# Attention in a planned order, a rearranged last routing chain, and fifteen weight halves loaded ahead

## The chip, the cores and the metric

The kernel runs on one core of a Trainium2 chip. It is one launch that holds a whole two-layer network for a batch of 16 images. The metric is device time in microseconds; the number of a kernel is the median over its runs. A profile is taken of one execution, and its times are counted from the start of that execution's span.

## The reference, cut to what matters

The input `x` has 16 samples of 128 channels x 32 x 32 points, so N = 1024 points per sample. All data are 32-bit floats.

```
x = x + attention(_ln_c(x))              # layer 0: 4 heads, linear attention:
                                         #   group norm over the sample, q,k,v = w_qkv xn
                                         #   q = softmax over points, k = softmax over channels of a head
                                         #   context = k v^T, out = context^T q, y = w_out out + b_out
t = tokens(x)
t = t + stu(_ln_t(t))                    # spectral filters (FFT convolution with K filters) + 3 taps,
                                         #   four lengths mixed by a softmax / one-hot of 4 weights
x = from_tokens(t)
x = x + relu(bn(conv3x3(relu(bn(conv3x3(_ln_c(x)))))) + residual)     # layer 1
t = tokens(x)
t = t + experts(_ln_t(t))                # 64 experts, each picks its 8 best of the 1024 tokens,
                                         #   pools them, 128 -> 512 -> 128 with a gelu,
                                         #   and adds its result back to those tokens
```

## The kernel before

The program goes through four stages, one after the other on the same core.

Stage A is the attention of layer 0 with all that the spectral part needs of each sample. A sample goes through some sixty named operations: `tokens` (TensorE turns x to tokens, eight 128x128 transposes, L152), `moments` and `root` and `scales` (mean and deviation per token, on DVE L135, ACT L121 and DVE L127 to L129), `norm` (ACT, L144, eight pieces), `channels` (TensorE turns back, L172), `channels_copy` (ACT L424), `group` (the group norm's scale, L402), `q` (L433) and `k` (L451) with their softmaxes, `q_tokens`, `context` (L499), `fold` and `fold2`, `out` (L534), `out_add`, `input` (L157), the second norm, `even` and `odd` (L571: the spectrum by even and odd parts), butterflies on POOL (L287 to L309) and the store of the spectrum `vd` (L628); beside it `taps_in`, `taps` (L639, 24 matmuls) and `taps_add` (L646), whose result is stored to `xd` (L647). The ACT copies between a TensorE result in PSUM and the next step are `tokens_copy` and `input_copy` (L550). In PSUM there are three buffers "big" (128x1024) and two "s" (small).

The order of A's work is written out by hand: `period` is a list of names with an offset each, and a loop over p from -6 to 15 issues every name for sample p + offset. TensorE, DVE, ACT and POOL execute in this order (their queues are pinned); the order on SP, which issues most DMAs, is left to the framework. Two generators are advanced once per period: `filters()` (the filters' own spectrum, L652 and L657, and the loading and mixing of M_phi) and `prepare()` (conv weights, on POOL). Where TensorE would be idle, `keep()` puts warm-up matmuls that compute nothing (L165):

```
idle = {("tokens", 1): 5, ("filters", 0): 4, ("channels", 0): 1, ("k", 1): 2}
```

At the start, DVE also prepares the taps' weights `mu` (L337, L339), whose DMA goes through POOL's queue.

Stage B is the spectral multiplication: per chunk of frequencies the samples' spectrum `xc` is fetched from `vd` (L793), turned on POOL, and multiplied with generated filters `g` (generate L817, copies L828 on DVE and L830 on ACT, multiply L841).

Stage C is the two convolutions. Its order comes from `planned()`, a list scheduler in the program: a table gives each operation an engine, a cost, a due time, what it depends on and the buffers it takes and frees; the scheduler issues the operation that is due and can run. Some operations of the last samples are moved by hand after that (`move`). Each sample ends in the routing of the experts: norm (`scales2`, `norm20`, `norm21`), `channels`, `logits` (L1320), the choice of eight tokens (L1341, L1344, for the last sample L1473 to L1485), the turning of the gates (`turn`, L1413 for the last sample, and its copy `turn_copy`), `pool` (L1367) and `pooled` (L1380, L1384). The last sample has a class of its own, `Final`, which works in halves. Conv's last steps on DVE and POOL are `sums2`, `ends2` (POOL L1222), `mids2` (L1226), `rows2` (L1232) and `last` (L1422, L1426).

Stage D is the experts. Of the 32 weight halves (1 MB each, 16 groups of experts with two halves) 14 are loaded ahead into a ring of tags whose buffers have become free (`RING`, `load_half`); half 2g+14 is issued after `hidden(g)` (L1684; biases before it, L1675) and half 2g+13 after `output(g-1)` (L1709), and behind the weights the five pairs of x that were put away (`AWAY`, xb) are reloaded. At the end the experts' outputs are turned (L1746), added up per pair of samples (`ob`, L1751), spread over the tokens with the gates (L1769, into `pfy`), added to x (L1779) and stored to the output.

Of the kernel before, what the change touches and what calls it, by code (L numbers as in the profile page):

```python
# [69 lines left out]
def metaformer_kernel(ctx: ExitStack, tc: tile.TileContext, io: dict, out: bass.AP):  # L70
# [106 lines left out]
    with ExitStack() as l0:  # L177
# [43 lines left out]
        with ExitStack() as a0:  # L221
            aconst = a0.enter_context(tc.tile_pool(name="aconst", bufs=1))
            setup = a0.enter_context(tc.tile_pool(name="setup", bufs=2))
            work = a0.enter_context(tc.tile_pool(name="awork", bufs=2))


            spool = a0.enter_context(tc.tile_pool(name="spool", bufs=2))
            xpool = a0.enter_context(tc.tile_pool(name="xpool", bufs=8))
            ppool = a0.enter_context(tc.tile_pool(name="ppool", bufs=1))
            ps = a0.enter_context(tc.tile_pool(name="aps", bufs=2, space=PSUM))  # L230
# [120 lines left out]
            def small(shape, name):  # L351
                return work.tile(shape, F32, name=name, tag=name, bufs=5)

            idle = {("tokens", 1): 5, ("filters", 0): 4, ("channels", 0): 1, ("k", 1): 2}

            class Attention:
# [10 lines left out]
                def tokens(self):  # L367
                    if self.b + 2 < B:
                        load(self.b + 2)
                    self.x = xt[self.b]  # L370
                    self.pt = big().rearrange("p (j c) -> p j c", c=C)
                    transpose_in(self.pt, self.x)

                def tokens_copy(self):
                    self.tok = work.tile([P, NT, C], F32, name="tok", tag="tok", bufs=3)
                    nc.scalar.copy(self.tok, self.pt)
# [171 lines left out]
                def input_copy(self):  # L548
                    self.ub = work.tile([P, NT, C], F32, name="ub", tag="ub")
                    nc.scalar.copy(self.ub, self.pt)  # L550
# [74 lines left out]
                def odd_turns4(self):  # L625
                    butterflies(self.ao, self.xf, 1, self.sd)
                    for cs in (slice(0, 1), slice(1, NCH)) if self.b + 1 == B else (slice(NCH),):
                        nc.sync.dma_start(  # L628
                            vd[cs, :, self.b, :].rearrange("c p w -> p c w"),
                            self.xf[:, cs].rearrange("p c x r m j -> p c (x r m j)"),  # L630
                        )
# [13 lines left out]
                def taps_add(self):  # L645
                    nc.vector.tensor_tensor(self.x, self.pa, self.x, ALU.add)  # L646
                    nc.sync.dma_start(xd[self.b], self.x)  # L647

            def filters():

                wfm = setup.tile([P, NQ // 2, 2 * P], F32, name="wfm", tag="mi")
                nc.vector.tensor_scalar(wfm, wf[:, 1::2, :], -1.0, None, ALU.mult)  # L652

                def values(q, dst):
                    for sgn in range(2):
                        w = wfm[:, q // 2, :] if sgn and q % 2 else wf[:, q, :]
# [4 lines left out]
                yield  # L661
                xf = spectrum_tile()
                for parity in range(2):
                    pe = class_values(parity, values)
                    t = class_copy(pe, 1)
                    ts = class_copy(pe, ROT) if parity else t
                    ab = class_sums(parity, pe, t)
                    class_differences(parity, ab, pe, ts)
                    yield
                    for part in range(2):  # L670
                        butterflies(ab, xf, parity, part)
                    if parity:
                        butterflies(ab, xf, 1, butterflies(ab, xf, 1, 2))
                    yield
                half = CW // 2
                e, o = (xf[:, :, i].rearrange("p c r m j -> p c (r m j)") for i in range(2))
                nc.vector.tensor_tensor(ph[:, :, :half], e, o, ALU.add)
                nc.vector.tensor_tensor(ph[:, :, half:], e, o, ALU.subtract)
                for m in range(EPR // MB):
                    es = slice(m * MB, (m + 1) * MB)  # L680
                    for i in range(NF):
                        mi = setup.tile([P, MB, C], F32, name="mi", tag="mi")
                        nc.sync.dma_start(mi, io["M_phi"][i, :, es, :])
                        yield
                        if i == 0:
                            nc.vector.tensor_scalar(mst[:, es, :], mi, coef[:, 0:1], None, ALU.mult)
                        else:
                            nc.vector.scalar_tensor_tensor(
                                mst[:, es, :], mi, coef[:, i : i + 1], mst[:, es, :], ALU.mult, ALU.add
                            )  # L690

            def prepare():
# [4 lines left out]
                for n in range(2):  # L697
# [20 lines left out]
                    for k, r, f in ((0, 0, 24.0), (1, 2, 6.0), (2, 1, 12.0)):  # L718
                        eng.tensor_scalar(cw[:, :, k], raw[:, :, r], 1.0 / f, None, ALU.mult)
                    eng.tensor_tensor(cw[:, :, 0], cw[:, :, 0], cw[:, :, 1], ALU.add)  # L720
# [4 lines left out]
                for n in range(2):  # L725
# [4 lines left out]
                    for si, (lo, hi) in enumerate(SEGS[1:], 1):  # L730
                        ws = w[:, :, :, lo // NQ : hi // NQ]
                        eng.tensor_scalar(ws, ws, seg[:, NF - 1 - si : NF - si], None, ALU.mult)
                        if si > 1:
                            yield
                    nc.sync.dma_start(wid[:, qs], w)

            nc.sync.dma_start(wf, io["wf"])
            phi = spool.tile([P, NQ, 2, P], F32, name="phi", tag="xf")
            nc.sync.dma_start(phi, io["phi"])


            period = (
                ("q_max", 3), ("out_add", 1), ("tokens", 6), ("moments", 6), ("context", 2),
                ("channels", 4), ("input", 1), ("norm2", 0), ("context_mask", 2),
                ("group_root", 4), ("k_exp", 3), ("fold", 2), ("group_scale", 4), ("moments2", 1),
                ("q_exp", 3), ("even", 0), ("tokens_copy", 6), ("taps_in", 0), ("input_copy", 1),
                ("channels_copy", 4), ("filters", 0), ("fold_copy", 2), ("even_copy", 0),
                ("even_sums", 0), ("taps_copy", 0), ("odd", 0), ("even_turns", 0),
                ("variance2", 1), ("root2", 1), ("q_tokens", 3), ("scales", 5), ("fold2", 2),
                ("q_copy", 3), ("k_sum", 3), ("scales2", 1), ("root", 6), ("spread", 5),  # L750
                ("k_recip", 3), ("k", 4), ("even_turns2", 0), ("q_recip", 3), ("variance", 6),
                ("fold2_copy", 2), ("odd_copy", 0), ("taps", 0), ("odd_sums", 0), ("k_max", 4),
                ("odd_scaled", 0), ("k_scale", 3), ("norm", 5), ("group", 5), ("odd_sums2", 0),
                ("q", 4), ("odd_turns", 0), ("taps_add", 0), ("odd_turns2", 0), ("out", 2),
                ("group_var", 5), ("odd_turns3", 0), ("k_sub", 4), ("odd_turns4", 0),
            )
            reach = max(d for _, d in period)
            samples, setting, preparing = {}, filters(), prepare()
            with tc.manual_schedule(engines=PINNED):
                for p in range(-reach, B):  # L760
                    next(preparing, None)
                    for name, d in period:
                        b = p + d
                        if name == "filters":
                            next(setting, None)
                            keep(ps, "s", idle.pop((name, 0), 0) if p > -reach else 0)
                        elif 0 <= b < B:
                            if name == "tokens":
                                samples[b] = Attention(b)
                            getattr(samples[b], "q_" if name == "q" else name)()  # L770
                            keep(ps, "s", idle.get((name, b), 0))
                assert next(preparing, None) is None
                for _ in setting:
                    pass
# [160 lines left out]
    with ExitStack() as c1:  # L935
# [12 lines left out]
            "y", "wi", "z", "y", "cw0", "v", "cw1", "p1", "yo",  # L948
        )
        FIRST = ("wi", "v", "cw0", "cw1", "p1", "y")  # L950
        halves = {}

        def load_half(h):

            g, n = divmod(h, 2)
            es, tag = slice(g * EG, (g + 1) * EG), RING[h % len(RING)]
            if g >= E // EG:
                pr = AWAY[0] + h - 2 * (E // EG)
                if pr in AWAY:
                    tag = RING[(pr - AWAY[0] + 18) % len(RING)]  # L960
                    pool = first if tag in FIRST else xpool if tag[:2] == "xp" else work
                    x = pool.tile([P, 2, N], F32, name=f"xb{pr}", tag=tag, bufs=RING.count(tag))
                    for j in range(2):
                        xt[2 * pr + j] = x[:, j]
                        nc.sync.dma_start(x[:, j], xd[2 * pr + j])
                return
            pool = first if tag in FIRST else xpool if tag[:2] == "xp" else work
            w = pool.tile([P, EG * HID], F32, name=f"we{n}", tag=tag, bufs=RING.count(tag))
            if n == 0:
                nc.sync.dma_start(  # L970
                    w.rearrange("p (e h) -> p e h", e=EG), w1[es, 0:C, :].rearrange("e d h -> d e h")
                )
            else:
                nc.sync.dma_start(
# [961 lines left out]
```

## Time and profile before

| what | value |
|---|---|
| median of 3 runs | 1227.47 us (1225.88 to 1232.86) |
| profiled execution | 1229.05 us, span 1227.0 us |
| granted TensorE clock, mean | 0.988 |
| stage A: last taps matmuls / last butterfly on POOL end | 384.1 / 386.65 us |
| taps of three samples in a row begin at (L639) | 194.98, 216.30, 237.63 us |
| first k matmuls (L451) | 29.22 us |
| first hidden layer of the experts (L1684) | 1137.65 us |
| last expert output matmuls (L1709) | 1192.81 us |
| first output store issued / last stores issued | 1202.81 / 1218.65 us |

PE is TensorE's matmuls and PEld its weight loads, DVE is VectorE, ACT is ScalarE, POOL is GpSimd and SP is SyncE. A line of a timeline has start, duration (all in us), engine, line in the program, operation, output and inputs by the program's names, sizes and how many such instructions stand together; the bracket tells how long the engine stood idle before it and what ended that. A wait line tells which engine waited for which work: us in total, how often, and the longest.

### The profile page before, as it was taken

The page shows a single profiled execution, that of the slowest core. Times are in us where ns is not written, and L with a number is a line of the kernel's source. Part 1 is how long each engine was busy: PE and PEld are TensorE (multiplying, and loading weights), DVE is VectorE, ACT ScalarE, POOL GpSimd, SP SyncE. Part 2 cuts the span into 40 slices and gives each one's busy share as a digit, 9 for nine tenths or more (in the row PEclk, how much of TensorE's full clock was granted, in tenths as well). Part 3 has the DMA queues.
Part 4 walks back from the last instruction along what each step waited for, and adds up shares of the span by engine and source line. Part 5 has one row for each costly group of instructions (what it writes and reads, how often), then busy time and mean ns, then how long its engine had stood idle before and what let it go on. Part 6 is the DMA issues. An engine that isn't in the chain of part 4 may idle for free.

```text
span 1227.0 us, 34351 instructions
## 1 busy us (share of the span) xinstructions
PE 1155.2 (94%) x14364; PEld 946.8 (77%) x14364; DVE 932.7 (76%) x1956; ACT 721.2 (59%) x1414; POOL 602.2 (49%) x800
## 2 busy tenths in 40 slices
PE   6889999999999999999997999999999999998996
PEld 4677767777677899998996888888888888885453
DVE  5888888887767677777764689898888989877335
ACT  4777777776656777877760445555555555554211
POOL 2436454664568788888882433343333333230003
PEclk9999999999999999999998999999999999999998
DMA  7004435243446244344348511233233322416998
GB/s 283 24 31 158 133 99 173 87 160 124 132 142 182 81 141 139 137 139 140 125 147 282 134 52 52 87 103 120 80 121 112 103 86 70 155 35 237 357 404 341
DMA packets 91243, 175.14 MB, mean 143 GB/s; under 512 B 5968, under 2 KB 42064, under 8 KB 90448
## 3 DMA queue, kind: packets, MB, share of 16 engines
q1 hardware_dynamic: 90448, 170.46, 41.1%
q0 software_dynamic: 640, 2.49, 0.6%
q8 instruction: 113, 1.85, 0.6%
q14 instruction: 42, 0.34, 0.1%
HBM read 110.28 MB, written 62.65 MB: 141 GB/s over the span
## 4 chain that ended last, share of the span: by engine, by line
PE 52%; DVE 22%; issue 10%; ACT 5%; DMA 5%; POOL 5%; SPq 0%; POOLq 0%; DVEq 0%; ACTq 0%
PE pcv L1013 10%; PE py L841 8%; PE pg L817 8%; PE big L639 6%; DVE bst L135 4%; PE big L172 3%; PE big L152 3%; PE big L571 3%; PE big L451 2%; PE big L534 2%; PE big L433 2%; DVE abss L1256 1%; DVE xp L1278 1%; DVE xp L1140 1%; POOL v L808 1%
## 5 line engine op out<-in xcount | busy, mean ns | idle before, releaser
L1013 PE MATMUL pcv<-v,cw 128*128 128x256 f32 x1152 | 258.2, 380 | 1.6 <-POOL v L1203 1.6
L1013 PEld LDWEIGHTS pcv<-v,cw 128*128 128x128 f32 x1152 | 214.7, 190 | 34.7 <-issue 4.9
L828 DVE COPY g<-pg 128x512 f32<-128x512 f32 x196 | 127.6, 682 | 67.9 <-PE pg L817 67.9
L830 ACT COPY g<-pg 128x512 f32<-128x512 f32 x316 | 161.1, 606 | 28.7 <-PE pg L817 27.9
L817 PE MATMUL pg<-ph,mst 32*128 32x128 f32 x4096 | 138.9, 278 | 1.4 <-DVE x L646 0.9
L817 PEld LDWEIGHTS pg<-ph,mst 32*128 32x128 f32 x4096 | 125.9, 187 | 15.6 <-DVE g L828 8.3
L841 PE MATMUL py<-g,v 128*32 128x128 f32 x4096 | 126.0, 276 | 1.9 <-POOL v L809 1.6
L841 PEld LDWEIGHTS py<-g,v 128*32 128x32 f32 x4096 | 109.2, 110 | 9.7 <-POOL v L809 2.1
L144 ACT ACTIVATE tok<-tok,sts 128x128 f32<-128x128 f32 x256 | 101.9, 480 | 16.9 <-DVE sts L1090 13.6
L135 DVE BATCH_NORM_STATS2 bst<-big 128x6 f32<-128x256 f32 x252 | 89.6, 416 | 19.9 <-PE big L152 10.7
L808 POOL TENSOR_TENSOR v<-xc 128x256 f32<-128x256 f32 x128 | 98.0, 790 | 9.9 <-DMA xc<-vd 9.2
L639 PE MATMUL big<-u,mu 128*128 128x128 f32 (+4 forms) x384 | 86.0, 380 | 0.0
L1203 POOL TENSOR_TENSOR v<-abss 128x256 f32<-128x256 f32 x64 | 49.1, 787 | 68.2 <-DVE abss L1199 56.8
L287 POOL TENSOR_TENSOR xf<-ab 128x256 f32<-128x256 f32 x34 | 24.8, 728 | 112.6 <-DVE ab L254 112.5
L1222 POOL TENSOR_TENSOR yo<-abss 128x256 f32<-128x256 f32 x32 | 23.5, 734 | 107.5 <-DVE abss L1218 107.5
L639 PEld LDWEIGHTS big<-u,mu 128*128 128x128 f32 x384 | 56.7, 191 | 18.0 <-issue 15.4
L571 PE MATMUL big<-wf,ub 128*128 128x256 f32 x256 | 63.5, 392 | 0.2
L809 POOL TENSOR_SCALAR v<-v 128x256 f32<-128x256 f32 x64 | 55.0, 860 | 5.6
L476 POOL TENSOR_TENSOR ke<-ke,ks 128x1024 f32<-128x1024 f32 x16 | 30.6, 1913 | 54.9 <-DVE qs L484 43.2
L144 ACT ACTIVATE tt<-tt,sts 128x128 f32<-128x128 f32 x120 | 47.8, 481 | 13.9 <-DVE sts L1090 13.9
L571 PEld LDWEIGHTS big<-wf,ub 128*128 128x128 f32 x256 | 47.0, 193 | 9.1 <-ACT xn L424 3.0
L915 ACT COPY yt<-py 128x512 f32<-128x512 f32 x60 | 35.1, 585 | 31.2 <-ACT g L830 17.6
(277 smaller groups left out, 2479.8 us busy)
## 6 DMA issues: line engine op xcount, KB each, us to landing
we<-in_weight SPq DMA_DIRECT2D x32, 1024.0 KB, 9.1
xc<-vd SPq DMA_DIRECT2D x64, 256.0 KB, 3.0
yd<-ys SPq DMA_DIRECT2D x32, 512.0 KB, 3.6
vd<-xf SPq DMA_DIRECT2D x15, 1024.0 KB, 5.1
y<-yd SPq DMA_DIRECT2D x15, 896.0 KB, 6.1
x<-in_x SPq DMA_DIRECT2D x16, 512.0 KB, 5.5
mi<-in_M_phi SPq DMA_DIRECT2D x16, 512.0 KB, 4.7
xd<-x SPq DMA_DIRECT2D x16, 512.0 KB, 6.2
```

Source lines behind the costliest of these rows:

```text
L135: nc.vector.bn_stats(bst[:, j : j + 2, :].rearrange("p j s -> p (j s)"), src[:, j : j + 2, :].rearrange("p j c -> p c j"),)
L144: nc.scalar.activation(dst[:, j, :], src[:, j, :], AF.Identity, bias=nm[:, j : j + 1], scale=r[:, j : j + 1],)
L571: nc.tensor.matmul(dst, self.ub[:, q, :], wf[:, q, :], start=True, stop=True)
L639: nc.tensor.matmul(self.pa[:, a:hi], mu[:, NF - 1 - si, tap, :], self.u[:, a - tap : hi - tap], start=(tap == 0), stop=(tap == KU - 1),)
L808: nc.gpsimd.tensor_tensor(vv[:, x, 1:, bs], e, o, op)
L809: nc.gpsimd.tensor_scalar(v[:, :, 0, bs], v[:, :, 2, bs], -1.0, None, ALU.mult)
L817: nc.tensor.matmul(pg[r][:, i], mst[rs, 4 * q + i, :], ph[rs, c, :], start=True, stop=True,)
L828: nc.vector.tensor_copy(dst, src)
L830: nc.scalar.copy(dst, src)
L841: nc.tensor.matmul(py[rows, x, kl, :], v[:, (x * NM + m) * JL + jl, 1 - ri : 3 - ri, :] .rearrange("p k b -> p (k b)"), g[:, ((x * 2 + ri) ...
L1013: nc.tensor.matmul(pc[:, i], wt[:, dy, k, :], v[:, k, dy * WT : dy * WT + HT], start=(dy == 0), stop=(dy == 2),)
L1203: nc.gpsimd.tensor_tensor(v[:, k, WT : WT + HT], self.ab[:, 0], self.ab[:, 1], op)
```

## The change

Three stages are touched.

In stage A `period` and the two generators are replaced by the list scheduler of stage C, with a table of all operations of a sample, the filters' steps (`f_...`, now a class `Filters`) and the preparation's (`p_...`), and earliest times for the loads. All of A's warm-up matmuls go. The loads of x for samples 2 to 7 are issued at the start, interleaved with wf and phi: x0, x1, x2, x3, wf, x4, x5, phi, x6, x7. `tokens_copy` and `input_copy` are done in two halves. Small tiles have 7 buffers instead of 5. The last sample's spectrum store is one chunk on SP and 15 on ACT's queue, and its x is stored from ACT's queue too.

In stage C, `scales2` of sample 14 is done by POOL (six operations) instead of DVE (four) and is moved behind `ends2`; the copy of sample 13's turned gates is put ahead of sample 14's norm; the last sample's norm is four pieces on DVE and four on ACT instead of five and three. Of the seven warm-ups of two matmuls behind the last `logits` two are left, and the biases of the first two expert groups are put into PSUM there.

In stage D fifteen weight halves are loaded ahead. The added one lies in two quarters behind the halves in the tags "z" and "v". After that, whenever a half is used up, the next of a list is loaded: first all weights, then the five pairs of x. The four warm-ups of two matmuls behind the last transposes go. The first pair of samples is added and stored in halves of 512 points.

The diff, cut to its core:

```diff
-                    nc.scalar.copy(self.tok, self.pt)
+                    for h in range(2):
+                        js = slice(h * NT // 2, (h + 1) * NT // 2)
+                        nc.scalar.copy(self.tok[:, js], self.pt[:, js])
...
-            idle = {("tokens", 1): 5, ("filters", 0): 4, ("channels", 0): 1, ("k", 1): 2}
+            idle = {("begin", 0): 0}
...
-                    nc.sync.dma_start(xd[self.b], self.x)
+                    (nc.sync if self.b + 1 < B else nc.scalar).dma_start(xd[self.b], self.x)
...
+            for b in range(2, 4):
+                load(b)
             nc.sync.dma_start(wf, io["wf"])
+            for b in range(4, 6):
+                load(b)
             phi = spool.tile([P, NQ, 2, P], F32, name="phi", tag="xf")
             nc.sync.dma_start(phi, io["phi"])
+            for b in range(6, 8):
+                load(b)
...
-            period = (
-                ("q_max", 3), ("out_add", 1), ("tokens", 6), ("moments", 6), ("context", 2),
...
+            table = (
+                ("load", "SP", 1.28, 2153.3, "", "x", ""),
+                ("tokens", "PE", 0.88, 4110.1, "load", "big:t tok", ""),
+                ("moments", "DVE", 1.337, -1802.8, "tokens~.6", "", "big:t"),
+                ("tokens_copy", "ACT", 1.034, 110.7, "tokens moments~.7", "", "big:t"),
...
+                ("channels_copy", "ACT", 1.114, -1271, "channels group_scale", "xn", "big:c"),
+                ("q", "PE", 1.78, 1191.3, "channels_copy", "big:q", ""),
...
+                ("k", "PE", 1.8, -1013.3, "channels_copy", "big:k", ""),
...
+                ("taps", "PE", 5.22, 6831.9, "taps_copy", "big:ta", "u"),
...
+            order = planned(
+                table, buffers, B, 520.01, lambda b, name: b > 0 and name[:2] in ("f_", "p_"),
+                lambda b, name: START.get((b, name), START.get(name, 0.0)),
+            )
...
         RING = tuple(f"xp{pr}" for pr in AWAY) + (
-            "y", "wi", "z", "y", "cw0", "v", "cw1", "p1", "yo",
+            "y", "wi", "z", "y", "rest", "cw0", "v", "cw1", "p1", "yo",
         )
...
+        pending = [h for g in range(E // EG + 1) for h in (2 * g, 2 * g - 1)]
+        pending = [h for h in pending if len(RING) <= h < 2 * E // EG]
+        pending += [2 * E // EG + i for i in range(len(AWAY))]
...
-        idle = {(13, "turn"): 4, (13, "pooled"): 2, (15, "logits"): 7, (15, "turn"): 1}
+        idle = {(13, "turn"): 4, (13, "pooled"): 2, (15, "logits"): 2, (15, "turn"): 1}
...
+        class Other(Routed):
...
+            def scales2(self):
+                g = nc.gpsimd
+                r, a, t, nm = (self.sts[:, i, :] for i in range(4))
+                g.tensor_tensor(t, r, r, ALU.mult)
+                g.tensor_tensor(t, t, a, ALU.mult)
+                g.tensor_scalar(t, t, -0.5, 1.5, ALU.mult, ALU.add)
+                g.tensor_tensor(r, t, r, ALU.mult)
+                g.tensor_tensor(nm, self.m, r, ALU.mult)
+                g.tensor_scalar(nm, nm, -1.0, None, ALU.mult)
...
-        move((d, "scales2"), behind=(e, "mids2"))
+        move((d, "scales2"), behind=(e, "ends2"))
...
+        move((d - 1, "turn_copy"), ahead=(d, "norm20"))
...
+                if b == B - 1 and name == "logits":
+                    for g in range(2):
+                        phs[g] = ps.tile([P, HID], F32, name="ph", tag="cv", bufs=3)
+                    biases(0)
...
-                    load_half(2 * g + len(RING))
+                    freed(2 * g)
...
-            keep(ps, "cv", 4)
...
+                for hf in range(2 if pr == 0 else 0):
+                    cs = slice(hf * HALF, (hf + 1) * HALF)
+                    for b in range(2):
+                        nc.vector.tensor_tensor(xt[b][:, cs], py[b][:, cs], xt[b][:, cs], ALU.add)
+                        nc.sync.dma_start(outs[b][:, cs], xt[b][:, cs])
```

## Prediction

> **What bounds the kernel now.** I read the busy rows and the 40 slices first, then windows by stage, then the waits of one stretch and the timeline of single periods. The profiled execution took 1229.05 us, 1.6 above the median of the runs shown (1227.47); its span is 1227.0 and 2.05 us lie around it. Sums are made against 1229.05; 1.6 comes off at the end.
>
> ```profile
> PE 1155.2 (94%) x14364; PEld 946.8 (77%) x14364; DVE 932.7 (76%) x1956; ACT 721.2 (59%) x1414; POOL 602.2 (49%) x800
> PE   6889999999999999999997999999999999998996
> DMA  7004435243446244344348511233233322416998
> ```
>
> TensorE has work for 94% of the span; DMA fills its slices only at the very end. So there are two regimes: up to about 1140 us TensorE's order and its holes set the pace, after that the transfers do.
>
> Stage A (attention) ends with the last taps matmul at 384.1 and POOL's last butterfly at 386.65. By windows (columns: window, length, busy time and count of PE, weight loads, DVE, ACT, POOL, then clock, DMA share, GB/s):
>
> ```profile
> 0.00:80.00 80.00, 64.34 (x405) 46.62 (x406) 59.39 (x191) 52.75 (x110) 25.55 (x36) 0.98 0.34 123
> 120.00:248.00 128.00, 123.94 (x862) 94.84 (x858) 106.61 (x260) 95.50 (x200) 66.51 (x104) 1.00 0.40 127
> 335.00:385.00 50.00, 47.69 (x268) 36.00 (x266) 33.25 (x62) 24.92 (x50) 34.90 (x61) 1.00 0.47 149
> 195.00:216.30 21.30, 20.62 (x144) 15.77 (x143) 17.86 (x43) 15.89 (x34) 11.71 (x18) 1.00 0.43 133
> ```
>
> One period is 21.3 us with 20.62 of TensorE work: the steady state has no more than 0.7 us per sample to give. The poor part is the ramp: 15.7 us idle in the first 80 and the 64.3 busy contain 10.3 us of warm-up matmuls (24 at 0.43) that compute nothing. The steady hole is one wait:
>
> ```profile
> 210.48 1.09 PE L172 MATMUL big<-ident,ub 128*128 128x128 f32 x8 [0.67 <-ACT ub L550]
> PE big L172 <- ACT ub L550: 9.2, 11, 1.6
> ```
>
> At the end:
>
> ```profile
> 1128.24 3.29 PE L165 MATMUL wm<-ident 128*128 128x256 f32 x14
> 1131.89 1.05 PE L1675 MATMUL ph<-b,ident 32*32 32x512 f32 x4
> 1192.81 1.08 PE L1709 MATMUL peo<-we,ht 128*32 128x128 f32 x32 [1.63 <-DMA we<-in_weight]
> 1196.71 2.76 PE L165 MATMUL wm<-ident 128*128 128x256 f32 x8
> 1195.00:1200.00 5.00, 4.94 (x18) 3.94 (x20) 2.16 (x8) 0.00 (x0) 0.00 (x0) 0.66 1.03 420
> 1200.00:1205.00 5.00, 5.00 (x23) 2.09 (x20) 3.45 (x3) 1.01 (x1) 0.55 (x1) 1.00 0.53 217
> ```
>
> Warm-up matmuls stand in line with the last routing chain; the last weight half is waited for 1.63 us; the transfers run full until 1200 and then only half full for 5 us, since the first output is not yet added up. From 1205 on 8.4 MB of outputs at about 400 GB/s are the rest (21 us).
>
> **Part 1, stage A in a planned order: −17 us.**
> *Work that stays.* All matmuls of the samples remain: 16 x 20.65 (123.94 over 6 periods) = 330.5, and the filter values, two groups of 16 (3.69 us each) = 7.4; together 338.
> *Work that goes.* 24 warm-ups, 10.3 us. They fill idle time at the ramp, so the gain comes only where real work takes their place:
> *Ramp.* The first transposes run at 7.5 in both (x lands then). The four mu operations stay where they hold DVE until mu lands (before: L337 at 14.04, the last L339 ends at 17.0), then scales, norm on ACT (3.2), channels (1.7) and the group's scale; the first k, at 29.22 before, comes at about 26.5, because the filters' sums no longer lie in front of the first sample's scales (DVE L254, L267, 20.43 to 21.7). Of the 19 us up to there TensorE has about 8.5 of useful work (10.5 lost); 6 more are lost, I estimate, until enough samples are in flight: 16.5 (before: 15.7 and 10.3 of warm-ups in 0:80). So 7.5 + 16.5 + 338 = 362.
> *Small stalls.* Busy time in A (0 to 385) is 356.7 in all; less the 10.3 it is 346.4, 8 above 338, since lone matmuls show their latency. In a denser stream I keep some of it: +5. TensorE ends at 367 instead of 384.1, and POOL's last butterfly 2.5 behind as before. So −17. If the ramp loses nothing beyond the start, and no stall stays: −27. If it keeps before's 0.67 per sample and the ramp is no better than 20 lost: about −8.
> *Other queues.* SP now issues x2 and x3 ahead of wf, and x4, x5 ahead of phi; before the phi landed at 15.95 and its matmuls waited for it (0.80). Four loads of 0.5 MB at 400 GB/s put it 5 us later, at 21; the values (3.7) stand ahead of the first k in TensorE's queue and end at 24.7, before k's input: 0, and +2 in the range if phi is later. If mu (on POOL's queue, 9.6 us to land before) is slowed by this traffic, DVE's whole queue stands behind it, x0's scales and norm first: 0 to +3, in the range; I take 0, as x's loads ran beside it before too. The two ACT copies per sample are each split in halves: 32 more instructions (1024-wide 1.01, 512-wide 0.58: 0.3 per sample on an engine busy 15.9 of 21.3): nothing while TensorE leads, and the half that comes first lets its reader begin earlier. Seven small buffers for five only remove waits.
> *The seam.* For the last sample vd's other 15 chunks and x's store go onto ACT's queue: two issues of about 0.4 us ahead of g's copies, which wait for POOL's last butterfly in both programs; 0 to +1, taken as 0.5 and contained in the 5. xc's first three fetches now stand behind vd's first chunk on SP (before they were issued at 380.43, ahead of it), but the fourth (xc at 391.61, 5.45 to land) came last before as well: 0, with ±2 in the range.
>
> *A rule against it.* Granted clock with the warm-ups: 0.98 in 0:80; after the waits of 1190 to 1195, 0.66 in 1195:1200. The Trainium skill (TensorE: Matmul & The Clock Gate, Part 1: The HAM clock gate) says that TensorE is granted only half its clock until it has been busy for some 3.4 us. By the rule, dropping the warm-ups makes the first transposes, the 3.7 us of filter values and the first k groups slower, up to +4 us at the ramp, and A gives −13. The row's 0.98 says nothing for a program without them. I take +1, inside the 5, since the first work after the transposes waits for mu and phi anyway; +4 stays in the range.
>
> **Part 2, last routing chain: −2.75.** Of the warm-ups behind the last logits (14 matmuls, 3.29 us from 1128.24, 0.235 each) 4 remain (0.9), and the 16 bias matmuls of the first expert pair (4 x about 0.27 = 1.05) come here, where TensorE waits for the exp and the gates (DVE L1485 ends at 1131.2) anyway. In before the flips follow at 1131.37, and the bias group of 1.05 stands between the two flips, 12 more (1.07) behind the pooling. Gone from the path: 0.75 of warm-ups past the gates' end or its latency, 0.85 between the flips, 0.45 before ppt = 2.05.
> Scales2 of sample 14 leaves DVE: four operations, 1112.71 to 1113.45 = −0.74 on the engine that carries the chain (mids, rows, last, moments). It becomes six POOL operations, with no row but the kin L1294:
>
> ```profile
> L1294 POOL TENSOR_SCALAR sts<-bst x16: 196/250/1095, 726.4 to 1120.0; 128x8 f32<-128x8 f32 x16
> 1109.09 1.09 POOL L1294 TENSOR_SCALAR sts<-bst 128x8 f32<-128x8 f32 x1 [8.55 <-DVE bst L135]
> ```
>
> By the median 6 x 0.25 = 1.5, from ends2's end at 1111.81 to 1113.3: norm of sample 14 on ACT begins about where it did (1113.57). The long one of 1.09 lay beside a DVE operation with two inputs in SBUF (L1344, 1108.92 to 1110.13). The Trainium skill (GPSIMD Engine Reference, 8. Key points) has POOL share SBUF interfaces with VectorE and contend with such operations; mids, rows and last are of that kind. By the rule each of the six may be held: up to 6 x 1.09 = 6.5, end at 1118.3, norm (3.19) ends at 1121.5, channels (1118.94) would start 2.5 late and its copy would hold ACT before the final norm. I go by the median and keep +2.5. Gtt's copy ahead of norm20 stands in that order on ACT already (1111.38 and 1113.57): 0. Four and four instead of five and three in the final norm: ACT starts when DVE's last is written (1.80 <- L1444), 4 x 0.336 + 4 x 0.39 = 2.9 against 2.83: 0.
>
> **Part 3, experts and outputs: −4.95 more.** The DMA stream of weights and x reloads sets the end from 1145 on (400 to 420 GB/s, share 1.05). It starts 2.75 earlier, and 1 MB is loaded ahead of it: at (15, inverse), when the slices show DMA at 0.4, into tiles that are free; 1 MB at 405 GB/s = 2.6. And the 2.35 us hole (5 us at 0.53) closes: TensorE's 8 warm-ups (2.76, 1196.71 to 1199.47, beside which DVE's ob sums run until 1199.1) go, the first pair is added and stored in halves, so the first store is issued about 1195 (before's clock) instead of 1202.81. With part 2: 2.75 + 2.6 + 2.35 = 7.7. The expert chain of TensorE (hidden 0 at 1137.65 to outputs at 1193.9, less the 1.63 wait, moved by 2.75) ends at about 1189.5, the added part (ot, ob, first half pair) some 6 us later: 1195.5, just when the stream ends. All weights now go ahead of all x reloads, which are needed from the second pair on, 3 us later: near, but covered. By the clock rule above, the first pair without warm-ups takes double (8 matmuls 1.99 and 1.88): +1.9. Range of parts 2 and 3: −3.5 to −9.
>
> **Sum.** −17 − 7.7 = −24.7: 1229.05 − 24.7 = 1204.35, less 1.6 = **1203**.
>
> **Rivals.** A measurement of this kernel tells about 0.5% (6.1 us): faster is below 1221.3, slower above 1233.6.
> 1. *The plan keeps holes.* Stage C's order comes from the same planner, and in 720:1060 TensorE waits 11 us of 340 (6.6 of them `PE big L172 <- DVE xp L1140`), 3.2%, just what A's hand-written period has (0.67 of 21.3). Then A gains only its ramp: −9; with 7.7, 1212.4, so **1211**. Against: in the new order each steady operation's input stands well ahead of it.
> 2. *The tail gives half.* Cold clock at the first pair or POOL held: parts 2 and 3 give −3.5 to −4, all in all −20.7: **1207**.
> 3. *Slower.* TensorE's queue is in order, with three "big" PSUM buffers between it and the ACT and DVE copies. In the planned order k follows the channels' copy, and fold the mask, with a few tenths of us; if the real copies come later than planned, TensorE stalls in every sample. It decides from 24.7/16 = 1.54 us per sample, a period of 22.2 against 20.65; at 2.3 per sample (16 x 2.3 = 36.8) **1239.5**. For: seven of the waits behind C's 6.6 us are of this kind. Against: DVE (17.9) and ACT (15.9) have 3 to 5 us free in a period.
> 4. *No change*: the same at 1.2 to 1.9 per sample, 1227.
>
> **Chances.** Forecast 0.60, rival 1 0.17, rival 2 0.10 (all faster: 0.87), no change 0.05, slower 0.08. Range: down to 1191 (A −27, tail −9: 1193, less 1.6), up to 1216 (rival 1 with the late mu and a cold ramp); no change and slower are left out.
>
> **What would show it.** Right: taps every 20.7 to 20.9 us from the fifth sample on, POOL's last butterfly near 369, the last L1709 near 1172 without a wait for we, DMA share near 1 through the first stores. Wrong: waits of L451, L433 or L571 on ACT or DVE in each period (rival 1 or 3); L1294-like POOL operations of 1 us and a late norm of sample 14; pfy at 1.9 for eight with a DMA share of 0.5 ahead of the first store (rival 2).

## The result, and the profile after

The changed kernel takes 1220.93 us in the median of 20 runs (1216.33 to 1227.12), the kernel before 1227.7 in 20 runs beside it (1224.04 to 1237.89). The ratio is 0.9932, with a 95% interval of 0.9914 to 0.995: faster by 8 us or so by the ratio, 7 by the medians, where the prediction had 25. The measured time lies above the top of the range (1216). The profiled execution took 1224.1 us with a span of 1222.0.

First the page of the changed kernel: busy times, then the slices of TensorE, of its granted clock and of the DMA engines.

```profile
PE 1145.7 (94%) x14322; PEld 941.2 (77%) x14322; DVE 943.2 (77%) x1953; ACT 727.2 (60%) x1447; POOL 604.7 (49%) x806
PE   6899999999998999999997899999999999998995
...
PEclk8999999999998999999998999999999999999997
DMA  7224463322234334444458311233233321416997
```

These are the clock row before, and the warm-up matmuls of the whole kernel before and after (count, busy us, mean ns, idle time):

```profile
PEclk9999999999999999999998999999999999999998
L165 PE MATMUL wm<-ident 128*128 128x256 f32 (+1 forms) x112 | 32.0, 436 | 0.0
L165 PE MATMUL wm<-ident 128*128 128x256 f32 x70 | 16.1, 382 | 0.0
```

TensorE lost 9.5 us of busy time (1155.2 before), though 15.9 us of warm-ups went, so its other work became 6.4 us longer; the span shrank by 5. The first digit of the clock row is 8 where it was 9. The windows of stage A (columns as in the prediction) show the later steady state full and the ramp not; the last line is from the kernel before:

```profile
0.00:20.00 20.00, 8.00 (x38) 7.08 (x39) 13.63 (x75) 10.67 (x26) 3.05 (x10) 0.85 0.85 321
20.00:40.00 20.00, 18.56 (x125) 15.47 (x123) 16.88 (x44) 16.19 (x40) 8.74 (x8) 0.89 0.42 150
40.00:80.00 40.00, 35.43 (x270) 25.09 (x270) 37.72 (x72) 28.18 (x53) 34.59 (x35) 1.00 0.25 82
120.00:248.00 128.00, 122.92 (x829) 94.69 (x825) 116.35 (x265) 96.50 (x209) 59.22 (x96) 0.99 0.47 150
248.00:335.00 87.00, 87.00 (x626) 68.33 (x625) 66.94 (x162) 63.85 (x133) 45.34 (x78) 1.00 0.25 79
248.00:335.00 87.00, 83.03 (x572) 62.80 (x569) 68.53 (x155) 58.97 (x119) 47.83 (x73) 0.98 0.41 132
```

In 248:335 TensorE is busy all the time, where before it was for 83.03 of 87. Between 120 and 248 it is idle for 5.1 us, 4%, so the steady state is not free of holes. The last taps end near 373.1 (384.1 before) and POOL's last butterfly at 374.6 (386.65): a gain of 11 to 12 us. These are the stages of the two kernels and of the eight below by one profile of each, in us ("old" means that stage A is the one of before; "gen" generates the filters and "mul" is the spectral multiplication, "hidden" the first hidden layer of the experts):

| kernel | A: last taps matmul begins | first gen to last mul | last conv to first hidden | hidden to first store | first store to end of span |
|---|---|---|---|---|---|
| before | 383.6 (old) | 259.6 | 27.8 | 65.2 | 24.2 |
| no_warm | 389.6 (old) | 256.5 | 27.9 | 62.5 | 22.8 |
| cd_only | 381.5 (old) | 262.2 | 26.6 | 62.2 | 25.4 |
| after | 372.6 | 262.9 | 26.6 | 62.7 | 26.1 |
| a_only | 372.6 | 264.1 | 28.2 | 67.2 | 24.0 |
| warm_end | 373.6 | 262.5 | 26.6 | 62.0 | 25.7 |
| warm_start | 370.4 | 266.7 | 26.7 | 61.7 | 25.5 |
| ring14 | 370.2 | 264.2 | 26.7 | 61.7 | 25.9 |
| seam | 372.7 | 258.2 | 26.6 | 62.7 | 26.1 |
| best | 371.6 | 260.0 | 26.6 | 61.7 | 26.1 |

One execution of one kernel differs from another by some us in a stage, so the columns are read over several rows. Stage A gave about 11 us. Of these, 4 to 5 went again in the spectral multiplication (first gen to last mul). The last routing chain gave 1.4. The output stage gave 0.7 us by the means, which is not clear of noise, since the three old ones differ by 6.

### The profile page after: what moved, and what is told of

It is laid out like the page before. It is cut to its first block, busy times and chain, and to the rows that moved or that the text cites. A ratio compares the mean times of both kernels' runs of the same rounds, so it can differ in the third digit from the quotient of the medians.

```text
span 1222.0 us, 34375 instructions
## 1 busy us (share of the span) xinstructions
PE 1145.7 (94%) x14322; PEld 941.2 (77%) x14322; DVE 943.2 (77%) x1953; ACT 727.2 (60%) x1447; POOL 604.7 (49%) x806
## 4 chain that ended last, share of the span: by engine, by line
PE 47%; DVE 27%; issue 11%; ACT 5%; DMA 5%; POOL 4%; SPq 0%; POOLq 0%; DVEq 0%; ACTq 0%
PE pcv L1211 10%; PE pg L987 9%; PE py L1011 9%; DVE bst L135 4%; PE big L573 3%; PE big L152 3%; PE big L172 3%; PE big L643 3%; DVE abss L1454 1%; DVE xp L1476 1%; PE big L534 1%; DVE xp L1338 1%; PE big L451 1%; DVE sts L128 1%; ACT tt L144 1%
## 5 line engine op out<-in xcount | busy, mean ns | idle before, releaser
L1011 PEld LDWEIGHTS py<-g,v 128*32 128x32 f32 x4096 | 109.0, 111 | 12.5 <-POOL v L978 2.8
L144 ACT ACTIVATE tok<-tok,sts 128x128 f32<-128x128 f32 x256 | 101.9, 481 | 15.9 <-DVE sts L1288 13.6
L144 ACT ACTIVATE ub<-ub,sts 128x128 f32<-128x128 f32 x128 | 50.8, 479 | 8.9 <-DVE sts L566 8.9
```

The costliest lines, as they stand in the source:

```text
L144: nc.scalar.activation(dst[:, j, :], src[:, j, :], AF.Identity, bias=nm[:, j : j + 1], scale=r[:, j : j + 1],)
L1011: nc.tensor.matmul(py[rows, x, kl, :], v[:, (x * NM + m) * JL + jl, 1 - ri : 3 - ri, :] .rearrange("p k b -> p (k b)"), g[:, ((x * 2 + ri) ...
```

## The experiments

All ratios are to the kernel before, run on the same chip: 1229.39 us (39 runs) beside `a_only`, `cd_only`, `seam` and `warm_end`, 1230.73 us (23 runs) beside the other four.

**The two halves of the change.** `a_only` has stage A of the changed kernel and everything behind it as before; `cd_only` the reverse.

```diff
# a_only: the block of stage A as changed
# cd_only: this block as before, all behind it as changed
-        with ExitStack() as a0:      # period, generators, warm-ups
+        with ExitStack() as a0:      # table, planned(), Filters
```

> Stage A of the changed kernel, stages B, C and D as before: how much of the change lies in part 1. By the two traces A ends 12.05 us earlier (POOL's last butterfly 374.6 against 386.65) and 4 to 4.5 of it are given back at the seam to stage B, since three fetches of xc stand behind the last sample's store. Theory: about 7.5 us faster than before, 0.994. Rival (the packed order itself gave 17 as predicted, and the changed kernel lost it later): 0.986.

Measured: 1225.61 us (18 runs), 0.9966 (0.9952 to 0.998).

> Stage A and B as before, stages C and D of the changed kernel: parts 2 and 3 alone. By the two traces the last routing chain gives 1.2 and the first expert layer to the first store 2.5, and 1.9 of that go again in the output stage at a lower granted clock. Theory: 1 to 3.5 us faster, 0.997 to 0.999. Rival (the predicted 7.7 are there and the profiled execution hid them): 0.994.

Measured: 1225.06 us (22 runs), 0.9963 (0.9948 to 0.9978).

Together they are 0.71%, and the whole has 0.68%: the parts add up, and there is no sign that either hid what the other gave (each ratio is uncertain by 0.15%, 1.8 us). Of 1229 us, part 1 gives 4.2 where the prediction had 17, parts 2 and 3 give 4.5 where it had 7.7. The theory for `a_only` (0.994) lies a little outside the interval, its rival (0.986) far outside. For `cd_only` the theory's near end (0.997) is inside, and the rival (0.994) is not.

**The seam between A and B.** In the changed kernel POOL waits after its last butterfly (timeline of POOL, changed kernel):

```profile
374.16 0.45 POOL L309 TENSOR_TENSOR xf<-sd 128x128 f32<-128x128 f32 x1
381.55 1.43 POOL L978 TENSOR_TENSOR v<-xc 128x256 f32<-128x256 f32 x2 [6.94 <-DMA xc<-vd]
383.06 0.85 POOL L979 TENSOR_SCALAR v<-v 128x256 f32<-128x256 f32 x1
```

and the queue of SP says why: seven fetches of xc are issued behind the first chunk of the last sample's store, which itself waits for that butterfly.

```profile
374.63 0.32 SPq L632 DMA_DIRECT2D vd<-xf  x1
375.04 12.94 SPq L963 DMA_DIRECT2D xc<-vd  x7
```

Before, three of the fetches had been issued at 380.43, 6 us ahead of the butterfly's end, and POOL went on to the first xc at 386.60 without a wait:

```profile
380.43 6.07 SPq L793 DMA_DIRECT2D xc<-vd  x3
386.60 1.42 POOL L808 TENSOR_TENSOR v<-xc 128x256 f32<-128x256 f32 x2
397.13 1.43 POOL L808 TENSOR_TENSOR v<-xc 128x256 f32<-128x256 f32 x2 [2.87 <-DMA xc<-vd]
```

The experiment puts that chunk beside the other fifteen on ACT's queue:

```diff
-                        (nc.scalar if cs.start == 1 else nc.sync).dma_start(
+                        (nc.scalar if self.b + 1 == B else nc.sync).dma_start(
```

> The changed kernel, with the last sample's first vd chunk on ACT's queue beside the other 15, so that SP's queue has the xc fetches next. Theory (POOL's 6.94 us wait for xc at 374.6 is caused by the three fetches standing behind this store; with them there POOL turns the first three xc at once, and the fourth lands last as before): first full multiply 3 to 3.5 us earlier behind POOL's last butterfly (13 instead of 16.3), total -3 to -3.5. Rival (POOL's turning of all four is bound by the landing of the fourth only): 0, the wait moves behind the third.

Measured: 1216.73 us (6 runs), 0.9885 (0.9852 to 0.9919); the ratio of the changed kernel is 0.9932, so this is some 5.8 us better, with an uncertainty of 4.7 by the two intervals. Kernels with the old store on the same chips agree: `warm_end` is at 1221.82 us beside `seam`, and `warm_start` at 1222.48 beside `best`, which has the new store and is at 1215.77 (these kernels, all below, differ in warm-ups too). In the trace of this kernel:

```profile
374.26 0.45 POOL L309 TENSOR_TENSOR xf<-sd 128x128 f32<-128x128 f32 x1
374.67 1.42 POOL L978 TENSOR_TENSOR v<-xc 128x256 f32<-128x256 f32 x2
...
383.45 1.42 POOL L978 TENSOR_TENSOR v<-xc 128x256 f32<-128x256 f32 x2 [1.76 <-DMA xc<-vd]
```

POOL turns the first three xc right behind the butterfly, and waits 1.76 us for the fourth instead of 6.94 for the first. The first full group of 64 multiplications begins at 387.20, against 390.94 for what was left of it in the changed kernel. The rival (bound by the fourth fetch in any case) falls. From the end of the last butterfly to the first long multiplication it is 16.3 to 16.9 us in the five profiles that have the new stage A and the store on SP, 12.5 in `seam` and in `best`, and 12.9 to 13.9 in the three with the old stage A. In the table, first gen to last mul falls from 262.5 to 266.7 (five kernels with the new stage A and the store on SP) to 258.2 and 260.0 (`seam`, `best`), which is the range of the kernels with the old stage A (256.5 to 262.2). By these means (264.1 and 259.1) the seam cost 5 us, some 4 of them ahead of the first long multiplication; where the rest lies was not found.

**The clock in the output stage.** Four warm-ups of two matmuls go back in front of the last combination:

```diff
+            keep(ps, "cv", 4)
             for q in range(NPAIR):
```

> The changed kernel with the four warm-ups (8 matmuls) back in front of the last combination. Theory (the output stage lost time to the clock: pfy at 1056 ns instead of 589 for the first pair): pfy at 589 ns within 3 us, first store 1 to 2.5 us earlier, total -1 to -2. Rival (the warm-ups only push the first pair back by their 2.8 us, and the first store is bound by DVE's sums): 0 to +2.

Measured: 1221.82 us (6 runs), 0.9931 (0.9905 to 0.9958): no difference in time to the changed kernel, but the interval is too wide to tell the theory from the rival. The changed kernel's first pair, and that of `warm_end` (timelines of TensorE):

```profile
1193.06 2.89 PE L1989 MATMUL pfy<-gt,ob 64*128 64x512 f32 x5 [0.40 <-DVE ob L1971]
1194.94 1.06 PE L1989 MATMUL pfy<-eg,ob 64*128 64x512 f32 x1
```

```profile
1186.90 1.89 PE L165 MATMUL wm<-ident 128*128 128x256 f32 x8
1188.85 2.02 PE L1990 MATMUL pfy<-gt,ob 64*128 64x512 f32 x7
1190.67 0.59 PE L1990 MATMUL pfy<-eg,ob 64*128 64x512 f32 x1
```

In the changed kernel a matmul takes 1.06 us, with the warm-ups 0.59. The warm-ups are not the only way to that: `ring14` and `warm_start` have none here, and their profiles show 0.59 too, where `cd_only` and `seam` show 1.06. From the first hidden layer to the first store it is 62.7 us in the changed kernel and in `seam`, 61.7 in `ring14` and `warm_start`, and 62.0 with the warm-ups. So the slow first pair costs up to 1 us and is there in three of five profiles without warm-ups; the warm-ups take 0.3 themselves. That cannot be told in the times.

**The clock in the ramp.** Five warm-ups are put where TensorE waits 4.59 us for DVE:

```diff
-            idle = {("begin", 0): 0}
+            idle = {("begin", 0): 0, ("tokens", 2): 5}
```

> The changed kernel with five warm-ups (10 matmuls of 128x512) behind the third sample's transposes, where TensorE waits 4.59 us for DVE (17.85). Theory (the ramp ran at a lower granted clock, 0.85 and 0.89 in 0:20 and 20:40, and the values, transposes and channels between 18.3 and 24.5 took some 3 us longer than later ones): these at full speed, first k at 24 to 25 instead of 26.7, the last taps 1 to 3 us earlier than 372.6. Rival (the ramp is bound by DVE and ACT behind it, so TensorE only waits longer there): last taps within 0.5 us of 372.6, total 0.

Measured: 1222.48 us (11 runs), 0.9946 (0.9921 to 0.997). In its trace the theory holds up to the end of stage A. The clock of the first 20 us is 1.00, the first k begins at 24.72 (26.69 in the changed kernel), and the last taps at 370.4 instead of 372.6. But no gain is seen in time; by the two intervals one of more than 2 us is excluded. Why the 2.2 us are lost behind stage A was not found.

`ring14`, below, has no warm-up there, and yet its clock row is 1.00 from the start, k came at 25.4 and the last taps at 370.2. That is not all due to the ramp. At 153 us `ring14` was 0.7 us ahead of the changed kernel (`warm_start` 2.1). Another 1.3 came at one hole, where TensorE waits for DVE's sums for the group's scale. Here is that hole in the changed kernel (first fence) and in `ring14` (second):

```profile
156.41 0.38 PE L402 MATMUL pg<-gt,avg 128*128 128x1 f32 x2 [2.17 <-DVE gt L398]
156.66 2.91 PE L573 MATMUL big<-wf,ub 128*128 128x256 f32 x8
159.36 1.82 PE L152 MATMUL big<-ident,qe 128*128 128x128 f32 x8
```

```profile
155.72 0.38 PE L402 MATMUL pg<-gt,avg 128*128 128x1 f32 x2 [2.16 <-DVE gt L398]
155.96 1.97 PE L573 MATMUL big<-wf,ub 128*128 128x256 f32 x8
157.77 1.04 PE L152 MATMUL big<-ident,qe 128*128 128x128 f32 x8
```

The wait is the same, and the same work behind it is slower in the changed kernel: the granted clock in 155:160 is 0.75 there and 1.00 in `ring14`. The other five profiles with the new stage A have the hole too, and 0.66 to 0.77. From the transposes ahead of the hole to the same ones of the next period it is 23.9 us in these six and 22.5 in `ring14`. So the new order has a hole in the steady state that cost 1.3 us more than its 2.2 in six of seven profiles.

**The old order without its warm-ups.**

```diff
-            idle = {("tokens", 1): 5, ("filters", 0): 4, ("channels", 0): 1, ("k", 1): 2}
+            idle = {("tokens", 1): 0, ("filters", 0): 0, ("channels", 0): 0, ("k", 1): 0}
```

> The kernel before without the 24 warm-up matmuls of stage A, its order unchanged. Theory (they lie in waits and keep the clock up): 10.3 us of busy time go and the last taps end no earlier, 0 to 3 us later, total 0 to +3. Rival (they stand in the way of real work): last taps up to 4 us earlier.

Measured: 1227.75 us (12 runs), 0.9978 (0.9958 to 0.9998). In its profile stage A ends 6 us later (389.6), twice the most that the theory had. The first 16 k matmuls took 3.79 us instead of 2.05, and the windows show a lower clock, first in the kernel before, then without the warm-ups:

```profile
20.00:40.00 20.00, 16.36 (x85) 11.21 (x84) 12.44 (x39) 14.66 (x33) 4.02 (x7) 1.00 0.32 110
40.00:80.00 40.00, 35.12 (x277) 26.26 (x276) 36.84 (x98) 31.73 (x66) 16.52 (x17) 0.96 0.09 29
20.00:40.00 20.00, 13.64 (x64) 10.89 (x62) 11.03 (x33) 11.95 (x29) 4.03 (x7) 0.74 0.33 112
40.00:80.00 40.00, 33.42 (x225) 26.05 (x225) 33.26 (x91) 31.50 (x66) 16.55 (x17) 0.87 0.06 19
```

The total is nevertheless not slower. Both expectations fail on it: the theory's later end of stage A is there, its later end of the kernel is not. The profiled execution (span 1228.8) made up for the late stage A in stage B (256.5) and in the outputs (22.8, no late weight half), the shortest of all. Why the kernel is not slower over all its runs stays open.

**Fourteen halves again.** The fifteenth half goes; weights still come ahead of the x reloads (the edit is cut to its core).

```diff
-            "y", "wi", "z", "y", "rest", "cw0", "v", "cw1", "p1", "yo",
+            "y", "wi", "z", "y", "cw0", "v", "cw1", "p1", "yo",
```

> The changed kernel with 14 weight halves loaded ahead instead of 15; the order of weights before x reloads stays. Theory (the megabyte shortens the stream, but what it saves falls into the hole ahead of the first store, which TensorE and DVE set): first store within 1 us of 62.7 after the first expert layer, the hole 2 to 2.6 us smaller, total 0 to +1. Rival (the predicted price, 2.6 us for the megabyte): +2.6, from the first expert layer to the end 91.4 instead of 88.8.

Measured: 1222.19 us (7 runs), 0.9932 (0.9903 to 0.9962), the ratio of the changed kernel to the fourth digit. The times alone do not exclude the rival's 2.6 us, since their difference is uncertain by 4. The windows do better. In the changed kernel the low clock of the first pair is mixed in (0.64 to 0.68 in 1190:1200), so the fair partner is `warm_start`: fifteen halves, no warm-ups here, full clock. The lines are the 3 us ahead of the first store and the 6 us behind it, `warm_start` (first fence) and `ring14` (second):

```profile
1189.60:1192.60 3.00, 2.22 (x11) 1.12 (x12) 1.63 (x5) 0.00 (x0) 0.00 (x0) 1.00 0.46 187
1192.60:1195.60 3.00, 3.00 (x15) 1.44 (x12) 2.92 (x4) 1.01 (x1) 0.11 (x1) 1.00 0.69 268
1195.60:1198.60 3.00, 3.00 (x17) 2.34 (x16) 2.15 (x3) 1.01 (x1) 3.00 (x2) 1.00 0.64 257
```

```profile
1190.00:1193.00 3.00, 2.22 (x10) 1.02 (x11) 1.69 (x6) 0.00 (x0) 0.00 (x0) 1.00 1.02 418
1193.00:1196.00 3.00, 3.00 (x14) 1.52 (x11) 2.87 (x5) 1.01 (x1) 0.02 (x1) 1.00 0.95 380
1196.00:1199.00 3.00, 3.00 (x17) 2.26 (x15) 2.15 (x3) 1.01 (x1) 3.00 (x2) 1.00 0.84 333
```

With fifteen halves the loads are done early, and the DMA engines then stand partly empty (0.46, 0.69, 0.64). With fourteen they are full until 1193.07, when the first store is issued, and hardly less than full after that. The first store comes 61.7 us behind the first hidden layer in both, and the end of the span 87.2 (`warm_start`) and 87.6 us (`ring14`) behind it; the rival had 91.4. So the megabyte is worth little or nothing here. What sets the end is now the chain of the experts up to the first store, 62 us, and the 8.4 MB behind it.

**All remedies together.** `best` has the store of `seam`, the warm-ups of `warm_start`, one warm-up ahead of the last expert output and two behind the last transposes.

```diff
+            idle = {("begin", 0): 0, ("tokens", 2): 5}
...
+                        (nc.scalar if self.b + 1 == B else nc.sync).dma_start(
...
+                    if g == ng:
+                        keep(ps, "cv", 1)
...
+            keep(ps, "cv", 2)
```

> The changed kernel with the whole last vd store on ACT's queue, the five warm-ups at the start, one warm-up ahead of the last expert output and two behind the last transposes. Theory (seam, cold ramp and cold output stage each cost what the profiles show: 5, 1 to 3 and 1 to 2 us): 6 to 9 us below the changed kernel, 0.986 to 0.988 of before. Rival (only the seam counts): as the kernel with that alone, 0.9885.

Measured: 1215.77 us (5 runs), 0.989 (0.986 to 0.992). It is nearest the rival: no gain over `seam` (0.9885) is shown, though the interval also holds the theory's 0.986 to 0.988. So `seam`, one condition away from the changed kernel, is the smallest edit that beats both kernels.

## Why the prediction was wrong

The direction was right, and the size was not. By the two halves, part 1 gave 12.8 us less than its 17: about 6 are missing at the end of stage A and 5 at the seam, and 2 are not located. Parts 2 and 3 gave 3.2 less than their 7.7. Point by point, by the prediction's own steps:

- *Ramp, first k at 26.5.* It came at 26.69 in the profile of after, and that is luck. Its input was ready at 26.00 (the copy of L424), and the filter values, which the sum had ending at 24.7, ended at 26.69, slowed by the clock; in the other six profiles with the new stage A k came at 24.7 to 26.0. Idle time of TensorE up to the last taps' end is 25.6 us (24 in the sum), which is luck as well: 18.0 in the first 80 us, where the sum had all of its 24, and 7.6 behind them, where it had none.
- *Work that stays, 338, and small stalls, +5.* This term is the first that failed. TensorE was busy 347.5 us up to 373.1, 4.5 more than the 343 of the sum, and 346.1 in `ring14`, whose clock row was full. Before, busy time less the warm-ups was 346.4. So the denser order took nothing off the busy time; the sixteen-fold period was too small a measure of it. Before, a matmul of 120:248 stands for 0.144 us of busy time (123.94 for 862), one of all stage A without the warm-ups for 0.150 (346.4 for 2310); why is not shown. The prediction should have kept the 346. `ring14` ends stage A at 370.7, the changed kernel at 373.1: these 2.4 of the missing 6 go with the lower clock of that profile, 0.7 up to 153 us and 1.3 at the hole of 154 us, where the sum had +1 for the ramp and nothing for a hole.
- *The seam, "0, with ±2".* This is the step that was reasoned wrongly. The sum saw that three fetches moved behind the last store and held that the fourth sets the end in any case. It left out POOL: each xc has to be turned there for 2.3 us (1.43 and 0.85, in order), and before, three of these four turns lay in the time in which the fourth xc was on its way. With all four behind the store, they follow one another at the end. The trace has 16.3 us from the last butterfly to the first long multiplication, against 12.9 before and 12.5 in `seam`. By the means of the table it cost 5 us. The experiment has shown the cause.
- *Last routing chain, −2.75.* It gave 1.4 by the table (last conv to first hidden, 26.6 to 26.7 against 27.8 to 28.2), and both of its terms were too large. Scales2 on POOL took 1.96 us in all (six operations of 0.20 to 0.39), and the norm began 0.03 us behind the last of them. The price by the median row, 1.5, was near; none of the six took 1.09, though the operation that had did so again at 1105.96 (L1492). (Of the DVE operations that the prediction feared here, rows2 is not of the kind: one of its inputs, pcv, lies in PSUM.) On DVE the step from the first mids2 to rows2 fell from 1.76 us (before) to 1.49 in the changed kernel, where the first mids2 took 0.71 us instead of 0.42, and to 1.21 in `cd_only`: 0.3 to 0.55 instead of 0.74. The warm-ups and biases gave 1.05 from the logits' start to the first hidden layer, instead of 2.05. The 0.85 between the flips did not come: from the first flip to the second it was 1.64 us before and is 1.79 now. The second waits for a copy on ACT, which turns to the experts' biases first, and it did so before too: the bias matmuls there filled this wait. First the kernel before, then the changed one:

```profile
1131.37 0.60 PE L1413 MATMUL big<-ident,eg 128*128 128x128 f32 x4
1133.01 0.42 PEld L1413 LDWEIGHTS big<-ident,eg 128*128 128x128 f32 x4 [0.98 <-ACT gtt L1489]
```

```profile
1127.27 0.66 PE L1624 MATMUL big<-ident,eg 128*128 128x128 f32 x4 [0.24 <-DVE eg L1696]
1129.06 0.66 PE L1624 MATMUL big<-ident,eg 128*128 128x128 f32 x4 [1.14 <-ACT gtt L1700]
```

- *Experts and outputs, −4.95.* This step failed too. The wait for the last weight half is gone in all seven profiles with the new stage D, `ring14` among them, so the fifteenth half is not needed for that. It was 1.63 us in the profile of before, 2.56 in that of `a_only` and absent in that of `no_warm`, so with the old order it is not there in every execution. The megabyte at 2.6 failed, since its price holds only while the stream is what is waited for. The hole was to close and grew instead: the first store came 61.7 to 62.7 us behind the first hidden layer where the sum had 60, and it has been the bound since. Up to 1 us of this is the slow first pair, for which the prediction had 1.9 in its range. From hidden to the end of the span the old output stage needs 85.3 to 91.2 (three profiles), the new one 87.2 to 88.8 (seven): 0.7 us less by the means, and less spread. `cd_only` gained 4.5 us in time, and the stages account for 2 of them; the rest is not located.

Rival 1 (holes in the plan) had stage A's gain at 9 and the total at 1211, and is nearest in stage A. But its cause, waits in the steady state, is only part: 5.1 us in 120:248 (2.2 of them in the hole of 154 us), none in 248:335. Rival 2 gave parts 2 and 3 half, 3.5 to 4, and `cd_only` measured 4.5. Neither rival had the seam. Its ±2 was in the range, but a range made up of the best case of one part and the mean of the others does not reach to where three parts fail together.

One difference stays open. In the changed kernel's profile the second group of the conv's matmuls waits 4.06 us for POOL, which had waited longer for its y, and then runs at the slow clock (7.13 us for 24 matmuls instead of 5.45); of the 7.7 us that the kernel was ahead at the first group, 3.6 are left behind this one. With the new stage A six of seven profiles have such a wait of 2.24 us or more (`warm_end` has 1.83), with the old one only one of three (`no_warm`, 3.69), the others 1.62 and 1.72. Three are too few: that the longer wait belongs to the change is not shown, nor that it doesn't. It would explain part of why `a_only` and the changed kernel are behind what their first stages give.

## What to carry to other kernels

When a transfer is moved behind another in its queue, do not only ask which transfer lands last: ask what the engine behind them does between the landings, since that work loses its cover. A saving of DMA time counts only as long as the stream is what the end waits for; find the hole behind it first. And work is not what a full period times the number of samples makes: take the busy time that the stage has, less what is removed.

## What the runs showed of the hardware that was not expected

The granted clock in the first 20 us differs between executions with nearly the same work: 0.84 to 0.86 in four profiles with the new stage A and no warm-ups (`after`, `a_only`, `seam`, `warm_end`), and 1.00 in a fifth (`ring14`). The row does not tell all: in `ring14`, too, eight transposes (L152, at 19.70) took 1.95 us, where `warm_start` has 1.07.

The conv's second group ran at the full clock (5.45 us) behind waits of 1.62 to 1.83 us, and slower (7.13 to 8.46) behind six of the seven waits of 2.24 to 4.06; behind that of 3.16 (`warm_start`) it ran at full speed. The hole in stage A at 154 us is of the same kind: behind a wait of 2.16 or 2.17 us the clock in 155:160 was 0.66 to 0.77 in six profiles and 1.00 in the seventh (`ring14`). A wait of some 2 us may thus cost TensorE 1.3 to 1.7 us more than it lasts, and whether it does differs between executions.
